# One transfer per tile for the spread C, B, dt and dt*u of a selective scan, with partition = 4 x channel + state

## The chip, the cores and the metric

The kernel runs on one core of one Trainium2 chip. Time is device time in microseconds of one execution, and the median of several executions is compared. The engines of the core are TensorE (PE, matrix products), VectorE (DVE), ScalarE (ACT), GpSimd (POOL), and SyncE (SP), which here only issues DMA transfers. All engines run at the same time, each its own instructions in order, and wait for each other through semaphores. The transfers move data between HBM and SBUF, the on-chip memory of 128 partitions, over 16 DMA engines.

## What is computed

Four layers over x of shape (4, 56, 56, 96). Layers 0 and 1 each contain a selective scan over the 56 x 56 = 3136 positions of an image, in four directions (rows, rows backwards, columns, columns backwards), with 192 channels and 16 states to a channel. Layers 2 and 3 are linear attention and a feed-forward block. The part that matters here is the scan of layer 1 (that of layer 0 differs in constants and in a weight per direction):

```python
x_dbl = jnp.einsum('bkdl,kcd->bkcl', xs, x_proj_w)
dts, Bmat, Cmat = jnp.split(x_dbl, [DTRANK, DTRANK + DSTATE], axis=2)
dts = jnp.einsum('bkrl,kdr->bkdl', dts, dt_w)
...
dt = jax.nn.softplus(dt + dt_bias[None, :, :, None])
dA = jnp.exp(jnp.einsum('bkdl,kdn->lbkdn', dt, A))
dBu = jnp.einsum('bkdl,bknl,bkdl->lbkdn', dt, Bs, u)
...
def step(h, inp):
    dA_l, dBu_l, C_l = inp
    h = dA_l * h + dBu_l
    return (h, jnp.einsum('bkdn,bkn->bkd', h, C_l))
```

For each channel d and state n, h is decayed by exp(dt*A), receives dt*u*B, and is summed over the states with weights C. dt and dt*u depend on the channel and the position only, B and C on the state and the position only.

## The kernel before

The scan works on chunks of 448 positions: 2 layers x 4 images x 4 directions x 7 chunks = 224 chunks. The 192 channels are two halves e of 96 (NE = 2), and a half is three groups g of 32 channels (NG = 3). The 16 states are four quarters q of four states (NQ = 4). A round is one (chunk, e, q), 8 to a chunk and 1792 in all. In a round a tile of 128 partitions holds 32 channels times 4 states, and its three groups g stand beside each other in the free dimension. The partition is 32*s + d for state s (the state is q + 4*s) and channel d.

So dt and dt*u must be copied to four partitions per channel, and B and C to 32 partitions per state. This goes through HBM. `rows` writes the projection, C in rows 0 to 15 and B in rows 16 to 31, into `cf`; `prepare` stores it as `cd` (L547). `park` (L506) stores dt (tile `dtc`) or dt*u (tile `duc`) of a chunk as `dd`, one transfer each. `spread` (L511) fills a tile `dt` or `du` for one e with four transfers of 32 partitions, and `fetch` (L528) fills a tile `cb` with C and B of one q with four more. Each of the four copies C and B of one state to 32 partitions. `cb` has five buffers, `dt` and `du` two each.

A round reads these tiles as follows. ACT makes `da` = exp(dt*A) (L654, three groups, scale by the column `na`). PE spreads B of the quarter into PSUM by a product with the constant `sel` (L597), and DVE multiplies `du` by it for groups 0 and 1 (L695); POOL does group 2 from `cb` (L690). DVE runs the three scans (L702). POOL multiplies by C (`hc`, L744), and PE adds up the four states with the constant `four` (L775). ACT copies the sums to Y (L782) and passes the last column of each scan on (`carry`, L667 and L672).

Beside the scans run lanes of other work (projections, convolutions, layers 2 and 3), one part of a lane at a time in gaps. Their loads (`get` L890, `window` L930) and stores go through SP too. The order on PE, ACT, DVE and POOL is the order of the program text. That of SP's transfers isn't written by hand; the framework's scheduler sets it. SP issues in that order, and a transfer that waits for a semaphore holds all behind it. In `prepare`, o counts rounds before the chunk's first round: `cd` at -9, `dtd` parked at -5, `dud` parked and the first dt spread at -4, the first du at -3, the second du and dt at 0, a fetch at each of -3 to 0.

Of the kernel before, what the change touches and what calls it, by code (L numbers as in the profile page):

```python
# [11 lines left out]
F32 = mybir.dt.float32  # L12
# [4 lines left out]
ALU = mybir.AluOpType  # L17
AX = mybir.AxisListType
# [4 lines left out]
C = 96  # L23
DI = 192
NS = 16
NE = 2
NG = 3
NQ = 4
# [4 lines left out]
CS = 448  # L33
# [48 lines left out]
def _in_blocks(w):  # L82

    u, z = w[..., :DI], w[..., DI:]
    return np.concatenate([u[..., :128], z[..., :128], u[..., 128:], z[..., 128:]], -1)


def lay_out(i):
    i = {k: np.asarray(v) for k, v in i.items()}
    c96, c128, w96, w128, q96, q128 = Cols(C), Cols(128), Cols(C), Cols(128), Cols(C), Cols(128)  # L90
    p0, p1 = "L0_conv_", "L1_conv_"

    for n in ("norm_w", "norm_b", "norm2_w", "norm2_b", "ffn_b2"):
        c96.add("0" + n, i[p0 + n][:, None])
    for n in (
        "dw_b bn1_g bn1_b bn1_m bn1_v pw_b bn2_g bn2_b bn2_m bn2_v ln_g ln_b fus_b fus_ln_g fus_ln_b"
    ).split():
        c96.add("1" + n, i[p1 + n][:, None])
    c96.add("1dw_w", i[p1 + "dw_w"].reshape(C, 9))
    for l in "23":  # L100
        c96.add(l + "bq", i[f"L{l}_attn_bqkv"][:C, None])
        c96.add(l + "bff", i[f"L{l}_attn_bff"][:, None])
        c96.add(l + "b2", i[f"L{l}_ffn_b2"][:, None])
        c128.add(l + "b1", i[f"L{l}_ffn_b1"].reshape(3, 128).T)

    scan = (
        (i[p0 + "ssm_xw"], i[p0 + "ssm_dtw"], i[p0 + "ssm_dtb"], i[p0 + "ssm_Alog"], i[p0 + "ssm_D"]),
        (
            i[p1 + "x_proj_w"],
            i[p1 + "dt_w"],  # L110
            i[p1 + "dt_b"],
            i[p1 + "A_logs"].reshape(4, DI, NS),
            i[p1 + "Ds"].reshape(4, DI),
        ),
    )
    wd = np.zeros((2, 4, 128, WD), np.float32)
    for l, (xw, dw, db, al, dd) in enumerate(scan):
        r = RANK[l]
        for k in range(4):
            t = xw[k].T  # L120
            m = np.zeros((128, NE, 2, 64), np.float32)
            m[:C, :, 0, :32] = np.concatenate([t[:, r + NS :], t[:, r : r + NS]], 1).reshape(NE, C, 32).swapaxes(0, 1)
            m[:C, :, 0, 32 : 32 + r] = t[:, :r].reshape(NE, C, r).swapaxes(0, 1)
            m[:, :, 1, :32] = m[:, :, 1, 32:] = m[:, :, 0, :32]
            wt = np.zeros((128, DI), np.float32)
            wt[32 : 32 + r] = dw[k].T
            bias = np.zeros((128, NE), np.float32)
            bias[:C] = db[k].reshape(NE, C).T
            a = al[k].reshape(NE, NG, 32, 4, NQ).transpose(3, 2, 0, 4, 1).reshape(128, -1)
            wd[l, k] = np.concatenate([m.reshape(128, -1), wt, bias, a], 1)  # L130
        c128.add(f"{l}D", dd.T.reshape(NE, C, 4).swapaxes(0, 1))
    c128.add("0dir", np.broadcast_to(i[p0 + "dir_w"], (128, 4)))
    c128.add("0b1", i[p0 + "ffn_b1"].reshape(3, 128).T)
    for n, v in (
        ("1conv_b", i[p1 + "conv_b"][:, None]),
        ("1conv_w", i[p1 + "conv_w"].reshape(DI, 9)),
        ("1g", i[p1 + "out_norm_g"][:, None]),
        ("1b", i[p1 + "out_norm_b"][:, None]),
    ):
        c128.add(n + "a", v[:128])  # L140
        c128.add(n + "b", v[128:])

    w96.add("0in", _in_blocks(i[p0 + "in_w"].T))
    w96.add("1in", _in_blocks(i[p1 + "in_proj_w"].T))
    w96.add("0w1", i[p0 + "ffn_w1"].T)
    w96.add("1pw", i[p1 + "pw_w"])
    f = i[p1 + "fus_w"].T
    w96.add("1fa", f[:C])
    w96.add("1fb", f[C:])
    w96.add("1out", i[p1 + "out_proj_w"])  # L150
    w = i[p0 + "out_w"].T
    w128.add("0outa", w[:128])
    w128.add("0outb", w[128:])
    w128.add("0w2", i[p0 + "ffn_w2"].T.reshape(3, 128, C).transpose(1, 0, 2))
    for l in "23":
        w96.add(l + "qkv", i[f"L{l}_attn_Wqkv"])
        w96.add(l + "ff", i[f"L{l}_attn_Wff"])
        q96.add(l + "w1", i[f"L{l}_ffn_W1"].T)
        q128.add(l + "w2", i[f"L{l}_ffn_W2"].T.reshape(3, 128, C).transpose(1, 0, 2))
    bqkv = np.stack([i[f"L{l}_attn_bqkv"] for l in "23"])  # L160
    cols = {"c96": c96, "c128": c128, "w96": w96, "w128": w128, "q96": q96, "q128": q128}
    arrays = {"x": np.ascontiguousarray(i["x"]).reshape(NB, L, C), "bqkv": bqkv, "wd": wd}
    arrays.update({k: v.array() for k, v in cols.items()})
    return arrays, {k: v.at for k, v in cols.items()}


class Net:
# [42 lines left out]
    def par(self, group, name):  # L210
        a, n = self.at[group][name]
        return self.tiles[group][:, a : a + n]
# [37 lines left out]
    def setup(self):  # L250
        nc, tc, const = self.nc, self.tc, self.const
        par = self.par
        self.tiles = {}
        for g in ("c96", "c128", "w128"):
            t = const.tile(list(self.aps[g].shape), F32, name=g)
# [8 lines left out]
        make_identity(nc, self.ident)  # L264

        self.four = const.tile([128, 32], F32, name="four")
        nc.vector.tensor_reduce(self.four, self.ident.rearrange("p (s d) -> p d s", s=4), AX.X, ALU.add)
        self.avg96 = const.tile([C, C], F32, name="avg96")
        nc.vector.memset(self.avg96, 1.0 / C)
        self.cen96 = const.tile([C, C], F32, name="cen96")  # L270
# [27 lines left out]
        w = const.tile([128, 4], F32, name="wts")  # L298
        m = const.tile([128, 1], F32, name="wmax")
        d = par("c128", "0dir")  # L300
# [5 lines left out]
        nc.vector.tensor_scalar(w, w, m, None, ALU.mult)  # L306

        self.cscale = const.tile([128, 4], F32, name="cscale")
        nc.vector.memset(self.cscale, 1.0)
        nc.vector.tensor_copy(self.cscale[:NS], w[:NS])  # L310


        self.skip = []
        for l in range(2):
            dv = par("c128", f"{l}D")[:C].rearrange("p (e k) -> p e k", e=NE)
            s = const.tile([C, NE], F32, name=f"dsum{l}")
# [5 lines left out]
            g = const.tile([C, NE, C], F32, name=f"skip{l}")  # L322
# [6 lines left out]
        for n, bias in (("bn1", "1dw_b"), ("bn2", "1pw_b")):  # L329
            s = const.tile([C, 1], F32, name=n + "s")  # L330
            t = const.tile([C, 1], F32, name=n + "t")
# [14 lines left out]
        with tc.tile_pool(name="stage", bufs=1) as st:  # L346

            self.sel = const.tile([128, NQ, 128], BF16, name="sel")
            parts = st.tile([128, 128], F32, name="parts")
            nc.vector.tensor_tensor(parts[:, :32], self.ident[:, 64:96], self.ident[:, 96:], ALU.add)  # L350
            nc.vector.tensor_tensor(parts[:, :32], parts[:, :32], self.ident[:, :32], ALU.add)
            for q in range(NQ):
                nc.vector.tensor_copy(
                    self.sel[:, q].rearrange("p (s d) -> p s d", s=4),
                    parts[:, NS + q : NS + q + 13 : 4].unsqueeze(2).to_broadcast([128, 4, 32]),
                )
            self.some = self.upper(self.tiles["w128"][:, :CS])
            self.minus = const.tile([128, 64], BF16, name="minus")
# [3 lines left out]
            t = st.tile([C, 2, 3, 128], F32, name="q96")  # L362
            nc.scalar.dma_start(t.rearrange("p l m f -> p (l m f)"), self.aps["q96"])
            nc.vector.tensor_copy(self.w1q, t, saturate=False)
            t = st.tile([128, 2, 3, C], F32, name="q128")
            nc.scalar.dma_start(t.rearrange("p l m f -> p (l m f)"), self.aps["q128"])
            nc.vector.tensor_copy(self.w2q, t, saturate=False)
            for n, l in enumerate("23"):
                t = st.tile([128, 3], F8, name="b1s")
                nc.vector.tensor_copy(t, par("c128", l + "b1"), saturate=False)  # L370
                nc.vector.tensor_copy(self.b1q[:, n, :], t)
                t = st.tile([C, 1], F8, name="b2s")
# [4 lines left out]
            t = st.tile(list(self.aps["w96"].shape), F32, name="w96")  # L377
# [15 lines left out]
            for n, l in enumerate("23"):  # L393
                f = st.tile([C, 3 * C], F32, name="qkvf")
                w = par("w96", l + "qkv")
# [9 lines left out]
            t = st.tile([C, C], F32, name="pws")  # L405
# [6 lines left out]
            for n, s in (("a", slice(0, 128)), ("b", slice(128, DI))):  # L412
                rows = s.stop - s.start
                y = self.small("wy" + n, rows, C, (out[:, s], par("w96", "1fb")))
                for l, p in ((self.wyg, "1g"), (self.wyb, "1b")):
                    t = const.tile([rows, C], F32, name="w" + p + n)
# [87 lines left out]
        self.nc.gpsimd.tensor_tensor(in_rows(ch.duc), in_rows(ch.dtc), u[:, :, lo : lo + CS // HS], ALU.mult)  # L504

    def park(self, t):  # L506
        d = self.dram.tile([NE, C, CS], F32, tag="dd", name="dd", bufs=6)
        self.nc.sync.dma_start(d.rearrange("e p t -> p e t"), t)
        return d

    def spread(self, t, d):  # L511

        for s in range(4):
            self.nc.sync.dma_start(t[32 * s : 32 * s + 32], d.rearrange("(g d) t -> d g t", d=32))

    def spread_dt(self, ch, e):
        ch.dt.append(self.sp.tile([128, NG, CS], F32, name="dt"))
# [10 lines left out]
    def fetch(self, ch, q):  # L528

        t = self.sp.tile([128, 2, CS], F32, name="cb", bufs=5)  # L530
        rows = ch.cd.rearrange("(k n) t -> n k t", k=2)
        for s in range(4):
            self.nc.sync.dma_start(t[32 * s : 32 * s + 32], rows[q + 4 * s].partition_broadcast(32))
        ch.cb.append(t)

    def prepare(self, ch, o):
# [835 lines left out]
```

## Time and profile before

| | |
|---|---|
| median of 3 runs | 8356.53 us (8340.41 to 8364.75) |
| profiled execution, its own time | 8364.46 us |
| its span, first to last instruction | 8362.7 us |
| mean granted TensorE clock | 0.898 |
| DMA packets of the SP queue | 942720, 1408.34 MB, 68.2% of 16 engines' span |
| HBM read, written | 1141.42 MB, 268.14 MB |
| SP waiting before L508 for dtc, for duc | 1158.7 us, 1042.4 us |
| SP waiting before L533 for hc (POOL L744) | 383.5 us |

The profile is of one execution. A line of the table of groups gives the source line, the engine, the operation, the tiles written and read, the count, then the busy time in us and the mean duration in ns, then the engine's idle time just before these instructions and what ended most of it. A line of waits names the engine and line that waited, what it waited for, and the total in us, the number of times and the longest. A line of transfers gives the count, the KB of one, and the median of the time from issue to landing.

### The profile page before, as it was taken

The page shows a single profiled execution, that of the slowest core. Times are in us where ns is not written, and L with a number is a line of the kernel's source. Part 1 is how long each engine was busy: PE and PEld are TensorE (multiplying, and loading weights), DVE is VectorE, ACT ScalarE, POOL GpSimd, SP SyncE. Part 2 cuts the span into 40 slices and gives each one's busy share as a digit, 9 for nine tenths or more (in the row PEclk, how much of TensorE's full clock was granted, in tenths as well). Part 3 has the DMA queues.
Part 4 walks back from the last instruction along what each step waited for, and adds up shares of the span by engine and source line. Part 5 has one row for each costly group of instructions (what it writes and reads, how often), then busy time and mean ns, then how long its engine had stood idle before and what let it go on. Part 6 is the DMA issues. An engine that isn't in the chain of part 4 may idle for free. (4 is left out here: it accounts for less than half of the span.)

```text
span 8362.7 us, 119228 instructions
## 1 busy us (share of the span) xinstructions
PE 7469.6 (89%) x33633; PEld 2721.6 (33%) x33633; DVE 7516.6 (90%) x9555; ACT 6109.8 (73%) x12807; POOL 7177.3 (86%) x3991
## 2 busy tenths in 40 slices
PE   7889888898889988898899979988899888998997
PEld 3333233232333223232322323333333333333344
DVE  5999999999998999999998999999999999999921
ACT  5778878776787768786777766777776777767736
POOL 4999989989998999899898998998888888889820
PEclk8899989899999989998898989988899888999986
DMA  5777777678766777677776777676766667666721
GB/s 154 179 188 189 203 179 182 167 175 199 178 174 170 172 188 181 172 177 184 177 175 167 174 185 176 166 170 172 186 166 162 166 173 182 167 160 167 175 57 48
DMA packets 944159, 1417.77 MB, mean 170 GB/s; under 512 B 169410, under 2 KB 936644, under 8 KB 942628
## 3 DMA queue, kind: packets, MB, share of 16 engines
q1 hardware_dynamic: 942720, 1408.34, 68.2%
q8 instruction: 264, 4.33, 0.2%
q14 instruction: 403, 3.30, 0.1%
q10 hardware_dynamic: 772, 1.80, 0.1%
HBM read 1141.42 MB, written 268.14 MB: 169 GB/s over the span
## 5 line engine op out<-in xcount | busy, mean ns | idle before, releaser
L702 DVE TENSOR_TENSOR_SCAN h<-da,h 128x449 f32<-128x449 f32 (+1 forms) x5376 | 5507.1, 1071 | 134.9 <-ACT da L654 79.3
L744 POOL TENSOR_TENSOR hc<-h,cb 128x1344 f32<-128x1344 f32 x1792 | 4884.8, 2726 | 598.8 <-DVE h L702 413.6
L654 ACT ACTIVATE da<-dt,na 128x448 f32<-128x448 f32 x5376 | 3353.1, 632 | 1143.2 <-DVE h L702 1104.4
L695 DVE TENSOR_TENSOR h<-du,b 128x448 f32<-128x448 f32 x3584 | 2019.6, 604 | 182.7 <-PE b L597 112.6
L775 PE MATMUL y<-hc,four 128*32 128x448 f32 x14336 | 1913.0, 609 | 17.8 <-POOL hc L744 17.4
L690 POOL TENSOR_TENSOR h<-du,cb 128x448 f32<-128x448 f32 x1792 | 1754.1, 979 | 141.4 <-DMA cb<-cd 110.1
L762 PE MATMUL y<-w,zeros 128*96 128x448 bf16 x4843 | 1354.0, 397 | 0.0
L597 PE MATMUL b<-cf,sel 128*128 128x448 bf16 x1792 | 680.2, 380 | 631.2 <-DVE h L695 626.6
L762 PEld LDWEIGHTS <-zeros 128*96 128x96 bf16 x4843 | 603.2, 135 | 1111.0 <-issue 965.1
L775 PEld LDWEIGHTS y<-hc,four 128*32 128x32 f32 x14336 | 294.2, 113 | 1182.5 <-issue 660.5
L433 PE MATMUL pp<-U,wd 96*128 96x448 f32 x896 | 664.5, 830 | 12.1 <-DMA U<-u 8.3
L771 PE MATMUL y<-Y,ident 96*96 96x448 f32 x672 | 542.9, 898 | 18.6 <-ACT Y L782 14.3
L919 PE MATMUL ps<-win,dg 64*64 64x220 f32 (+11 forms) x1998 | 547.3, 471 | 0.0
L479 PE MATMUL pp<-cf,wd 12*96 12x448 f32 (+1 forms) x896 | 476.2, 613 | 71.7 <-ACT dtc L489 47.6
L672 ACT COPY carry<-h 128x3 f32<-128x3 f32 x1536 | 301.9, 197 | 282.3 <-DVE h L702 276.2
L504 POOL TENSOR_TENSOR duc<-dtc,U 96x896 f32<-96x896 f32 x224 | 483.1, 2157 | 3.3 <-ACT dtc L491 3.3
L782 ACT COPY Y<-y 96x448 f32<-96x448 f32 x448 | 341.7, 763 | 77.7 <-PE y L775 76.8
L919 PEld LDWEIGHTS ps<-win,dg 64*64 64x64 f32 (+2 forms) x1998 | 239.7, 162 | 321.5 <-issue 289.0
L667 ACT COPY h<-carry 128x3 f32<-128x3 f32 x1536 | 280.2, 182 | 66.3 <-POOL hc L744 63.5
L489 ACT ACTIVATE dtc<-pp,wd 96x448 f32<-96x448 f32 x448 | 281.7, 629 | 31.3 <-PE pp L479 27.4
L597 PEld LDWEIGHTS <-sel 128*128 128x128 bf16 x1792 | 183.8, 103 | 336.1 <-issue 272.7
L827 PEld LDWEIGHTS ps<-avg,w 96*112 96x112 f32 (+2 forms) x1944 | 249.9, 193 | 108.1 <-issue 59.0
(427 smaller groups left out, 5933.9 us busy)
## 6 DMA issues: line engine op xcount, KB each, us to landing
cb<-cd SPq DMA_DIRECT2D x3584, 112.0 KB, 3.9
dt<-dd SPq DMA_DIRECT2D x1792, 168.0 KB, 4.3
du<-dd SPq DMA_DIRECT2D x1792, 168.0 KB, 4.1
dd<-dtc SPq DMA_DIRECT2D x224, 336.0 KB, 3.0
dd<-duc SPq DMA_DIRECT2D x224, 336.0 KB, 3.1
U<-u SPq DMA_DIRECT2D x112, 168.0 KB, 4.7
z<-w SPq DMA_DIRECT2D x56, 224.0 KB, 4.5
u<-w SPq DMA_DIRECT2D x56, 224.0 KB, 3.9
```

The costliest lines, as they stand in the source:

```text
L433: self.nc.tensor.matmul(ch.ps.rearrange("p (a b) -> p a b", b=HS), ch.par.wx[:, e], self.in_order(self.U[e], ch.orient, ch.c * CS, CS), st ...
L504: self.nc.gpsimd.tensor_tensor(in_rows(ch.duc), in_rows(ch.dtc), u[:, :, lo : lo + CS // HS], ALU.mult)
L597: self.nc.tensor.matmul(ps, self.sel[:, q], self.upper(ch.cf), start=True, stop=True)
L654: nc.scalar.activation(da[g][:, INNER], ch.dt[e][:, g], AF.Exp, scale=ch.par.na[:, e, q, g : g + 1])
L690: nc.gpsimd.tensor_tensor(tokens(hs[n])[:, 2], ch.du[e][:, 2], ch.cb[q][:, 1], ALU.mult)
L695: nc.vector.tensor_tensor(tokens(hs[n])[:, g], ch.du[e][:, g], bs[n], ALU.mult)
L702: nc.vector.tensor_tensor_scan(h[:, way], da[g][:, way], h[:, way], 0.0, ALU.mult, ALU.add)
L744: nc.gpsimd.tensor_tensor(hc, tokens(hs[n]), ch.cb[q][:, 0].unsqueeze(1).to_broadcast([128, NG, CS]), ALU.mult,)
L762: self.nc.tensor.matmul(self.y[:C], self.zeros, self.some, start=False, stop=False)
L771: nc.tensor.matmul(o, w, self.in_order(a, ch.orient, ch.c * CS, CS), start=True, stop=False)
L775: nc.tensor.matmul(self.y[32 * n : 32 * n + 32], self.four, hc[:, g], start=n == 3, stop=n == 3 or q == NQ - 1,)
L919: self.nc.tensor.matmul(o[:, a - r0 : e - r0, x0:x1], diag[:, tap], win[:, a + dy - lo : e + dy - lo, x0 + dx : x1 + dx], start=n == 0, st ...
```

## The change

In the tiles of a round the partition becomes 4*d + s. The state of q and s is still q + 4*s. The rows of `cd` are reordered so that those of one q stand together and C and B of one state are neighbours: row 8*q + 2*s is C, row 8*q + 2*s + 1 is B. So the eight rows of one q are one contiguous stretch of HBM, and one transfer repeats it 32 times to fill `cb`. `dd` is stored as [e, channel in group, group, position], so that the three groups of a channel are one contiguous row of 3 x 448 values; one transfer reads each row four times and fills `dt` or `du`. For this, `park` writes with three transfers, one for each group, where it wrote with one. The constants follow the new order: the projection's columns, A, `four`, `sel`, and `cscale`, whose weight must now fall on every second row (only layer 0 uses it, on C).

```diff
-            m[:C, :, 0, :32] = np.concatenate([t[:, r + NS :], t[:, r : r + NS]], 1).reshape(NE, C, 32).swapaxes(0, 1)
+            cb = np.stack([t[:, r + NS :], t[:, r : r + NS]], -1).reshape(NE, C, 4, NQ, 2)
+            m[:C, :, 0, :32] = cb.swapaxes(2, 3).reshape(NE, C, 32).swapaxes(0, 1)
...
-            a = al[k].reshape(NE, NG, 32, 4, NQ).transpose(3, 2, 0, 4, 1).reshape(128, -1)
+            a = al[k].reshape(NE, NG, 32, 4, NQ).transpose(2, 3, 0, 4, 1).reshape(128, -1)
...
-        nc.vector.tensor_reduce(self.four, self.ident.rearrange("p (s d) -> p d s", s=4), AX.X, ALU.add)
+        nc.vector.tensor_reduce(self.four, self.ident.rearrange("p (d s) -> p d s", s=4), AX.X, ALU.add)
...
-        nc.vector.memset(self.cscale, 1.0)
-        nc.vector.tensor_copy(self.cscale[:NS], w[:NS])
+        nc.vector.tensor_reduce(m, self.ident[:, : 2 * NS : 2], AX.X, ALU.add)
+        nc.vector.tensor_scalar(self.cscale, w, m, None, ALU.mult)
+        nc.vector.tensor_scalar(m, m, -1.0, 1.0, ALU.mult, ALU.add)
+        nc.vector.tensor_scalar(self.cscale, self.cscale, m, None, ALU.add)
...
-                    self.sel[:, q].rearrange("p (s d) -> p s d", s=4),
-                    parts[:, NS + q : NS + q + 13 : 4].unsqueeze(2).to_broadcast([128, 4, 32]),
+                    self.sel[:, q].rearrange("p (d s) -> p d s", s=4),
+                    parts[:, 8 * q + 1 : 8 * q + 8 : 2].unsqueeze(1).to_broadcast([128, 32, 4]),
...
     def park(self, t):
-        d = self.dram.tile([NE, C, CS], F32, tag="dd", name="dd", bufs=6)
-        self.nc.sync.dma_start(d.rearrange("e p t -> p e t"), t)
+        d = self.dram.tile([NE, 32, NG, CS], F32, tag="dd", name="dd", bufs=6)
+        for g in range(NG):
+            self.nc.sync.dma_start(d[:, :, g].rearrange("e d t -> d e t"), t[32 * g : 32 * g + 32])
         return d
 
     def spread(self, t, d):
 
-        for s in range(4):
-            self.nc.sync.dma_start(t[32 * s : 32 * s + 32], d.rearrange("(g d) t -> d g t", d=32))
+        rows = d.rearrange("d g t -> d (g t)").unsqueeze(1).to_broadcast([32, 4, NG * CS])
+        self.nc.sync.dma_start(t.rearrange("p g t -> p (g t)"), rows)
...
         t = self.sp.tile([128, 2, CS], F32, name="cb", bufs=5)
-        rows = ch.cd.rearrange("(k n) t -> n k t", k=2)
-        for s in range(4):
-            self.nc.sync.dma_start(t[32 * s : 32 * s + 32], rows[q + 4 * s].partition_broadcast(32))
+        rows = ch.cd[8 * q : 8 * q + 8].rearrange("(s k) t -> s (k t)", k=2)
+        self.nc.sync.dma_start(
+            t.rearrange("p k t -> p (k t)"), rows.unsqueeze(0).to_broadcast([32, 4, 2 * CS])
+        )
         ch.cb.append(t)
```

## The prediction

> **What bounds the kernel now.** I read the page from the top: busy shares first, then the groups of part 5, the DMA issues of part 6, and after that the waits and the SP queue's timeline at the worst wait. The first two parts name the engine that sets the pace.
>
> ```profile
> PE 7469.6 (89%) x33633; PEld 2721.6 (33%) x33633; DVE 7516.6 (90%) x9555; ACT 6109.8 (73%) x12807; POOL 7177.3 (86%) x3991
> ...
> L702 DVE TENSOR_TENSOR_SCAN h<-da,h 128x449 f32<-128x449 f32 (+1 forms) x5376 | 5507.1, 1071 | 134.9 <-ACT da L654 79.3
> L744 POOL TENSOR_TENSOR hc<-h,cb 128x1344 f32<-128x1344 f32 x1792 | 4884.8, 2726 | 598.8 <-DVE h L702 413.6
> ...
> L695 DVE TENSOR_TENSOR h<-du,b 128x448 f32<-128x448 f32 x3584 | 2019.6, 604 | 182.7 <-PE b L597 112.6
> ...
> L690 POOL TENSOR_TENSOR h<-du,cb 128x448 f32<-128x448 f32 x1792 | 1754.1, 979 | 141.4 <-DMA cb<-cd 110.1
> ...
> cb<-cd SPq DMA_DIRECT2D x3584, 112.0 KB, 3.9
> dt<-dd SPq DMA_DIRECT2D x1792, 168.0 KB, 4.3
> du<-dd SPq DMA_DIRECT2D x1792, 168.0 KB, 4.1
> dd<-dtc SPq DMA_DIRECT2D x224, 336.0 KB, 3.0
> ```
>
> The scan stage has 1792 rounds. A round without a wait runs 4.0 us on DVE (two products of 0.6 us and three scans of 1.07 us, their ends overlapping), so 1792 x 4.0 = 7170 us of the 8363 us are DVE work of the scan alone. The view by windows says how much of the stage is idle:
>
> ```profile
> 200.00:2000.00 1800.00, 1595.13 (x7163) 546.43 (x7155) 1725.83 (x2153) 1393.93 (x2828) 1668.01 (x925) 0.90 0.74 183
> 2000.00:4000.00 2000.00, 1770.90 (x7919) 596.62 (x7911) 1898.22 (x2367) 1498.12 (x3006) 1837.18 (x1014) 0.91 0.73 180
> 4000.00:6000.00 2000.00, 1804.57 (x8171) 639.40 (x8172) 1881.74 (x2377) 1472.29 (x3121) 1802.62 (x999) 0.90 0.71 174
> 6000.00:7900.00 1900.00, 1761.08 (x8063) 653.65 (x8061) 1770.01 (x2262) 1374.75 (x3063) 1672.89 (x925) 0.91 0.69 169
> ```
>
> The columns are length, then busy time of PE, PE's weight loads, DVE, ACT and POOL, the clock, the DMA share and GB/s. DVE's busy time sums to 7275.8 of 7700 us, so DVE idles 424 us there. No change to transfers can win more than that, and only the part of it that ends on a transfer. The view of waits shows that part:
>
> ```profile
> DVE h L695 <- PE b L597: 112.6, 143, 4.6
> POOL h L690 <- DMA cb<-cd: 110.1, 28, 18.6
> ...
> DVE h L702 <- ACT da L654: 79.3, 165, 2.1
> ...
> DVE h L702 <- POOL h L690: 53.2, 26, 10.1
> ...
> DVE h L695 <- DMA du<-dd: 34.4, 9, 15.6
> ```
>
> DVE waits for du itself 34.4 us (15.6 of it once, at the first round), and 53.2 us for POOL's third product, which in its long cases had waited for cb. Three of those cases (10.1, 10.1 and 9.6 us, each followed by 2.0 us) come to 36 us; others at L702 are 1 us waits behind L1016 and L1017 on POOL. So transfers own some 70 us, at most 88 us, of DVE's idle time.
>
> Why are they late? One of the three cases, on SP and on POOL:
>
> ```profile
> 3532.66 0.47 SPq L930 DMA_DIRECT2D win<-m  x1
> 3533.23 1.95 SPq L514 DMA_DIRECT2D dt<-dd  x4
> 3535.27 1.78 SPq L533 DMA_DIRECT2D cb<-cd  x4
> ...
> 3540.63 0.98 POOL L690 TENSOR_TENSOR h<-du,cb 128x448 f32<-128x448 f32 x1 [13.25 <-DMA cb<-cd]
> ```
>
> SP issued nothing from 3517.4 to 3532.7: the window load of L930 at its head waited for a buffer. Only then came dt and cb, eight issues. POOL had been idle since 3527.4: 5.3 us before SP was free and 7.9 us after it, of which eight issues of 0.43 us are 3.4. The larger part is the queue's order and the landing, the smaller the number of issues.
>
> [...] of the packets of 1792 bytes a third take 70 to 75 ns, and from 200 to 7900 us the median is 113 ns and the 90th percentile 149[...]. [...] the scan takes 1054 to 1096 ns in every stage. So fewer bytes in flight buy nothing on DVE or POOL.
>
> **The change part by part.**
>
> *Issues.* Fetch: 3584 become 896. Spreads of dt and du: 2 x 1792 become 2 x 448. Park: 2 x 224 become 2 x 672. SP's 9000 transfers become 9000 - 2688 - 2688 + 896 = 4520. At the median of 0.43 us each (L533 and L514 by line), SP has 1.9 ms less to issue. That is not time on the path: SP also sits waiting for dtc and duc (1158.7 and 1042.4 us before L508). It counts only where a queue has built up.
>
> *Landing of a tile.* Now: the first to the last issue of the four is 1.29 to 1.6 us at the median for all but the first cb (which SP splits around a park), plus 3.9 to 4.3 us, so 5.2 to 5.9 us. After: packets of 3584 and 5376 bytes, eight on each engine. At the rate of the fast 1792-byte packet (74 ns) to that of the slow (149 ns), cb takes 8 x 148 to 298 ns = 1.2 to 2.4 us, dt and du 1.8 to 3.6 us. In today's 3.9 and 4.2 us are 4 and 6 packets of 114 ns, 0.46 and 0.68 us, so 3.45 to 3.5 us remain, part of it queueing behind other transfers. Together cb 4.65 to 5.85 us, dt and du 5.3 to 7.1 us: between 0.6 us earlier and 1.6 us later than now. I take no difference for cb and 0.5 us later for dt and du[...].
>
> *What slack hides that.* For each of the 224 chunks I set the last issue of a tile plus 4.2 us against the start of its first reader. Median slack is 4.5 us for the first cb, 4.6 for the second, 5.4, then 2.1 for the fourth; 6.6 for the first du, 11.4 for the second, over 7 for dt. So half a microsecond either way is hidden: summing what falls short, tiles that land 1 us later cost 20 us in all, 2 us 61, 3 us 142.
>
> *Backlogs.* Here issues count. At the first round DVE starts at 111.8 us after a run of 12 issues for du, dt and cb; three in their place save about 5 us. At 1683 us DVE waits 6.5 us for du, of which one quarter had been issued before the block and three after it; whole, it goes before: 4 us, as cb is next late. The three 12 us cases each keep the blocked window but have 6 issues fewer before the late cb, 6 x 0.43 = 2.6 us, 8 us in all. Near 1070, 2058, 3022 and 4000 us ten loads of the next lane and twelve spreads fill the queue; DVE waits there 1 to 2 us three times in a row, and L1016 on POOL waits for w; I take 3 us each, 12 us. The waits of 2.7 us near 1992 and 4926 us and small ones: 6 us. Sum 5 + 4 + 8 + 12 + 6 = 35 us. Bounds: 15 us if the lane's cases are POOL's own work, 80 us if SP's order also changes so that dt and cb pass the window load.
>
> *Park.* Two more issues before the last lands, 2 x 0.45 = 0.9 us later, and the spread behind it waits for three transfers. Queued behind on SP: dt, du and cb. The three spreads that follow now take 12 x 0.45 us and then 3, so this is covered; uncovered it is below the 20 us named above.
>
> *Semaphores.* Readers wait for one transfer where they waited for four: L690 has 2808 separate semaphore instructions on POOL, L695 1650 on DVE. They run while the engine is still busy: in the stage DVE's idle stretches under 100 ns sum to 2.5 us, POOL's to 2.4. Nothing gained.
>
> *Constants.* The new cscale is four small DVE operations in place of two in the set-up, under 1 us; `four` and `sel` keep shapes and counts, so L775 (609 ns) and L597 (380 ns) stay. Per-partition `na` and `cf` keep their form.
>
> Sum: the profiled execution has 8364.5 us (span 8362.7), so it becomes 8329; the median of the runs is 8 us below that execution, so 8321.
>
> **The rivals.**
> *Hidden anyway.* The long waits are order, not number; SP is idle half the time, and the median tile has 2 to 6 us of slack. Then only start and stray cases remain, 0 to 20 us: 8345. Against it speak the crowded stretches.
> *Slower: one transfer lands later than four.* Place: the fourth cb tile, slack 2.1 us. If [...]each tile waits for its slowest engine behind another 672 KB transfer, tiles land 2 us or more later: +61 us, at 3 us +142. It decides from about 2 us, where the loss of 61 us exceeds the 35 us won by 25 us. At 3 us, less the 35 won: 8357 + 107 = 8464. Against it: the range above ends at 1.6 us.
> *Not 16 engines.* [...]the 1.03 GB of the spreads and fetches (3584 x 112 KB + 3584 x 168 KB) through 4 engines at 24 GB/s (1792 bytes in 74 ns) would take 10.6 ms, beyond the whole span. [...]
>
> **How the numbers follow.** 0.3% is 25 us, about what a measurement of this kernel can tell. The 35 us case where it shows (25 to 80 us won, 8276 to 8331): 0.48. Hidden: 0.29. Slower: 0.21, and 0.02 for few engines. The predicted time is 8321. The likeliest case's own range, by its bounds of 15 and 80 us, is 8276 to 8341. The whole range goes to 8262, as all of DVE's waits for transfers (88 us) and a little of POOL's could go, and to 8420, which leaves out about half of the slower case.
>
> **What would show it.** SP transfers near 4520; cb, dt and du at 448 and 672 KB, landing in 4 to 6.5 us; the DMA share down from 68% to 45 to 60%; DVE's wait for du near 15 us and POOL's for cb near 60; durations unchanged. The window load still heads SP's queue in the three long cases. I am wrong if waits for cb spread over many chunks, if landings pass 7 us, or if DVE's idle time moves without transfers.

## The result and the profile after

The changed kernel takes 8281.9 us at the median (8280.05 to 8300.63, 4 runs) against 8360.64 us for the kernel before (4 runs): ratio 0.9918, 95% interval 0.9898 to 0.9938, so 0.82% faster (the quotient of the two medians, 0.9906, lies in the interval). The forecast was 8321 us, faster by 0.42%, with a range of 8262 to 8420. The profiled execution has 8300.6 us with a span of 8298.9 us, 63.8 us shorter than that of the kernel before.

The page of the changed kernel, its busy shares, its costliest groups and its transfers (the lines of the source have moved down by three to five: L695 is now the third product on POOL, L700 the products on DVE, L707 the scan, L749 the product with C):

```profile
PE 7409.9 (89%) x33633; PEld 2704.3 (33%) x33633; DVE 7512.5 (91%) x9557; ACT 6105.7 (74%) x12807; POOL 7176.7 (86%) x3991
...
q1 hardware_dynamic: 526976, 1408.05, 52.6%
...
L707 DVE TENSOR_TENSOR_SCAN h<-da,h 128x449 f32<-128x449 f32 (+1 forms) x5376 | 5501.9, 1070 | 93.5 <-ACT da L659 78.0
L749 POOL TENSOR_TENSOR hc<-h,cb 128x1344 f32<-128x1344 f32 x1792 | 4885.3, 2726 | 637.1 <-DVE h L707 502.8
...
L695 POOL TENSOR_TENSOR h<-du,cb 128x448 f32<-128x448 f32 x1792 | 1754.9, 979 | 44.8 <-DMA du<-dd 19.9
...
cb<-cd SPq DMA_DIRECT2D x896, 448.0 KB, 4.3
dt<-dd SPq DMA_DIRECT2D x448, 672.0 KB, 5.0
du<-dd SPq DMA_DIRECT2D x448, 672.0 KB, 5.6
dd<-dtc SPq DMA_DIRECT2D x672, 112.0 KB, 2.0
```

DVE and POOL work no less: DVE's busy time is 7512.5 us where it was 7516.6, POOL's 7176.7 where it was 7177.3, and a scan still takes 1.07 us. What changed is what stands after the last bar of a line, the idle time. That of L695 on POOL fell from 141.4 to 44.8 us. The same bytes keep the DMA engines busy for 52.6% of the span, not 68.2%.

PE's recorded busy time did fall, by 59.7 us, and this hints at a rival: the granted clock. It was 0.907 in the profiled execution where it was 0.898 before. In the four runs of the changed kernel it was 0.905 to 0.909, in the runs of the kernel before that stand beside the experiments below 0.896 to 0.904, and among those the quickest had one of the highest clocks (8319.91 us at 0.904) and the slowest one of the lowest (8376.52 us at 0.897). In the profiled pair the clock explains little, as DVE waits for PE's spread of B as long as before (112.6 us):

```profile
DVE h L700 <- PE b L602: 111.5, 135, 5.4
```

How much of the difference of the medians goes with the clock, and whether the clock is its cause or follows from it, stays open. No run held the clock fixed.

The waits of DVE in the changed kernel (engine and line, what it waited for, total, times, longest):

```profile
DVE h L700 <- DMA du<-dd: 22.0, 5, 17.9
...
DVE h L707 <- POOL h L695: 13.0, 15, 2.4
```

These answer to 34.4 and 53.2 us before. POOL itself waited 110.1 us for cb; now that line reads

```profile
POOL h L695 <- DMA cb<-cd: 0.3, 1, 0.3
```

and the wait at its first round, 19.9 us, is put down to du. In the stage from 200 to 7900 us (third of the busy times)

```profile
200.00:7900.00 7700.00, 6926.64 (x31603) 2441.48 (x31600) 7338.21 (x9241) 5784.09 (x12130) 7042.09 (x3895) 0.92 0.55 178
```

DVE's busy time is 7338.2 us of 7700 where it was 7275.8, so its idle time fell by 62.4 us, from 424.2 to 361.8. That is nearly the whole difference of the spans. Attributing each idle stretch of DVE in this stage to its releaser, du's own share falls from 18.8 to 4.1 us and that of POOL's third product from 53.7 to 13.4 us: 55 of the 62 us.

The three places where POOL had waited 13 us for cb behind a blocked window load are gone. SP at the second of them, in the changed kernel:

```profile
3505.28 0.51 SPq L518 DMA_DIRECT2D du<-dd  x1
3505.89 0.55 SPq L518 DMA_DIRECT2D dt<-dd  x1
3507.60 4.14 SPq L536 DMA_DIRECT2D cb<-cd  x2
3518.94 1.27 SPq L512 DMA_DIRECT2D dd<-dtc  x3
3525.58 0.30 SPq L512 DMA_DIRECT2D dd<-duc  x1
3525.98 0.49 SPq L935 DMA_DIRECT2D win<-m  x1
```

The second du, the second dt and the fetches of cb are issued first; the window load comes 18 us after the fetches begin, between the parts of a park. Before, the same load stood between du and dt and held dt and cb for 15 us. The change touches no window load. The scheduler that sets SP's order placed it elsewhere once the other transfers had changed.

So there are two candidates that the result alone doesn't tell apart: the order of SP's queue, which the change altered by accident, and the transfers themselves, fewer, larger, and over all 128 partitions.

### The profile page after: what moved, and what is told of

Its sections match the earlier page's. It is cut to its first block, busy times and chain, and to the rows that moved or that the text cites. A ratio compares the mean times of both kernels' runs of the same rounds, so it can differ in the third digit from the quotient of the medians.

```text
span 8298.9 us, 112395 instructions
## 1 busy us (share of the span) xinstructions
PE 7409.9 (89%) x33633; PEld 2704.3 (33%) x33633; DVE 7512.5 (91%) x9557; ACT 6105.7 (74%) x12807; POOL 7176.7 (86%) x3991
## 3 DMA queue, kind: packets, MB, share of 16 engines
q1 hardware_dynamic: 526976, 1408.05, 52.6%
## 5 line engine op out<-in xcount | busy, mean ns | idle before, releaser
L707 DVE TENSOR_TENSOR_SCAN h<-da,h 128x449 f32<-128x449 f32 (+1 forms) x5376 | 5501.9, 1070 | 93.5 <-ACT da L659 78.0
L749 POOL TENSOR_TENSOR hc<-h,cb 128x1344 f32<-128x1344 f32 x1792 | 4885.3, 2726 | 637.1 <-DVE h L707 502.8
L700 DVE TENSOR_TENSOR h<-du,b 128x448 f32<-128x448 f32 x3584 | 2017.1, 603 | 162.8 <-PE b L602 111.5
L780 PE MATMUL y<-hc,four 128*32 128x448 f32 x14336 | 1889.5, 602 | 19.0 <-POOL hc L749 18.5
L695 POOL TENSOR_TENSOR h<-du,cb 128x448 f32<-128x448 f32 x1792 | 1754.9, 979 | 44.8 <-DMA du<-dd 19.9
L767 PE MATMUL y<-w,zeros 128*96 128x448 bf16 x4843 | 1335.3, 393 | 0.0
L602 PE MATMUL b<-cf,sel 128*128 128x448 bf16 x1792 | 674.7, 377 | 632.2 <-DVE h L700 626.1
L780 PEld LDWEIGHTS y<-hc,four 128*32 128x32 f32 x14336 | 293.9, 112 | 1172.2 <-issue 676.7
L602 PEld LDWEIGHTS <-sel 128*128 128x128 bf16 x1792 | 183.3, 102 | 331.5 <-issue 267.6
```

Of the source, the lines that this page charges most:

```text
L602: self.nc.tensor.matmul(ps, self.sel[:, q], self.upper(ch.cf), start=True, stop=True)
L695: nc.gpsimd.tensor_tensor(tokens(hs[n])[:, 2], ch.du[e][:, 2], ch.cb[q][:, 1], ALU.mult)
L700: nc.vector.tensor_tensor(tokens(hs[n])[:, g], ch.du[e][:, g], bs[n], ALU.mult)
L707: nc.vector.tensor_tensor_scan(h[:, way], da[g][:, way], h[:, way], 0.0, ALU.mult, ALU.add)
L749: nc.gpsimd.tensor_tensor(hc, tokens(hs[n]), ch.cb[q][:, 0].unsqueeze(1).to_broadcast([128, NG, CS]), ALU.mult,)
L767: self.nc.tensor.matmul(self.y[:C], self.zeros, self.some, start=False, stop=False)
```

## The experiments

Every ratio is to the kernel before, with its 95% interval.

### Four issues for a tile again, but over 128 partitions

```diff
-        self.nc.sync.dma_start(t.rearrange("p g t -> p (g t)"), rows)
+        w = t.rearrange("p g t -> p (g t)")
+        for j in range(0, NG * CS, 336):
+            self.nc.sync.dma_start(w[:, j : j + 336], rows[:, :, j : j + 336])
```

`fetch` is cut in the same way into four times 224 columns.

> The changed kernel, but each tile of cb, dt and du is filled by four transfers again, each over all 128 partitions and a quarter of the columns (896 or 1344 bytes a row). SP issues 9896 transfers, more than before the change. If the gain came from the number of issues in SP's queue, it is lost: 8330 to 8370 us, and POOL waits for cb 60 us or more again. If it came from filling all 128 partitions at once ([...]shorter landing), it stays: 8275 to 8305 us.

Measured: 1.0013 (0.9998 to 1.0027). The whole win is lost, as the first of the two guesses had it. Its transfers and the waits at the third product:

```profile
cb<-cd SPq DMA_DIRECT2D x3584, 112.0 KB, 2.6
dt<-dd SPq DMA_DIRECT2D x1792, 168.0 KB, 2.8
du<-dd SPq DMA_DIRECT2D x1792, 168.0 KB, 2.9
```

```profile
POOL h L697 <- DMA cb<-cd: 88.0, 34, 19.9
```

```profile
DVE h L709 <- POOL h L697: 64.2, 55, 2.9
```

A transfer lands in 2.6 us where the kernel before needed 3.9, of as many bytes, and still POOL waits for cb and DVE for POOL. So a quicker single transfer doesn't hold the win when SP issues 9896 of them. DVE's wait also has another form: 55 short ones, none above 2.9 us, so the three long blocks are absent here too. This points to backlog in the queue. But number and price of the issues rose together: one of these takes SP 0.60 us at the median, where one of the kernel before took 0.43. The run doesn't separate the two.

### SP in the order of the program text, before and after

```diff
-    with tc.manual_schedule(engines={E.PE, E.Activation, E.DVE, E.Pool}):
+    with tc.manual_schedule(engines={E.PE, E.Activation, E.DVE, E.Pool, E.SP}):
```

The kernel before with this edit:

> The kernel before, with SP's transfers too in the order of the program text instead of the scheduler's. If the gain is that blocked window loads no longer stand ahead of dt and cb, text order alone gives most of it with the same 9000 transfers: 8290 to 8325 us and no wait of 10 us for cb. If it is the number of issues or the landing time, nothing comes of it: 8345 to 8375 us.

The changed kernel with it:

> The changed kernel, with SP in the order of the program text. If order is all, this equals e2 within 15 us. If the number of issues also counts at equal order, it stands 20 us or more below e2: 8265 to 8295 us.

Measured: 1.0039 (1.0017 to 1.0060) for the kernel before, 0.9989 (0.9980 to 0.9999) for the changed one. The guesses about text order missed: it helps neither kernel, and the kernel before is slower than either guess. Of the pair, the changed kernel is the faster by 43 us at the medians, in the direction of the second guess, but far from its 8265 to 8295 us. The traces in text order say why. First the changed kernel, on SP and then on DVE:

```profile
3502.43 19.36 SPq L935 DMA_DIRECT2D win<-m  x2
3521.89 0.55 SPq L518 DMA_DIRECT2D du<-dd  x1
3522.53 0.55 SPq L518 DMA_DIRECT2D dt<-dd  x1
3523.14 0.59 SPq L536 DMA_DIRECT2D cb<-cd  x1
```

```profile
3532.41 1.09 DVE L707 TENSOR_TENSOR_SCAN h<-da,h 128x449 f32<-128x449 f32 x1 [12.00 <-POOL h L695]
```

Then the kernel before, at the same place:

```profile
3532.38 17.54 SPq L930 DMA_DIRECT2D win<-m  x2
3550.03 1.94 SPq L514 DMA_DIRECT2D du<-dd  x4
```

```profile
3561.71 1.09 DVE L702 TENSOR_TENSOR_SCAN h<-da,h 128x449 f32<-128x449 f32 x1 [12.64 <-POOL h L690]
```

In text order the window load stands ahead of du, dt and cb in both kernels, and with one issue a tile the block costs nearly as much as with four: 12.0 us against 12.6 here, and 11.2 to 12.0 against 12.6 to 13.3 over the three places of this kind. So few issues don't cure a blocked head. At this common order the change still wins 0.5% (0.9989 to 1.0039).

### A fourth window buffer, so that nothing blocks

```diff
-NWIN = 3
+NWIN = 4
```

The kernel before with it:

> The kernel before with a fourth buffer for the window tile (NWIN 4), so that L930 need not wait for a buffer; SP still issues 9000 transfers in the scheduler's order. If the three waits of 12 us for cb behind a blocked window load were a main part of what the change won, they vanish and the time falls by 30 to 45 us, to 8305 to 8325 us at a before of 8350. If the number of issues is all, the time stays within 15 us of before.

The changed kernel with it:

> The changed kernel with the same fourth window buffer. If the change had already removed these waits by another way, nothing is left to win: within 10 us of the changed kernel, ratio to before 0.990 to 0.993. If blocked window loads still cost something, a further 15 to 40 us.

Measured: 0.9957 (0.9941 to 0.9972) and 0.9919 (0.9892 to 0.9946). The kernel before wins 0.43% from a buffer alone, some half of what the change won, and in the range expected. In its trace:

```profile
DVE h L702 <- POOL h L690: 18.4, 21, 2.4
DVE h L695 <- DMA du<-dd: 31.9, 9, 15.6
```

```profile
POOL h L690 <- DMA cb<-cd: 54.4, 20, 19.0
```

DVE's wait for POOL's third product falls from 53.2 to 18.4 us; that is 35 of the 38 us by which the median fell. POOL's wait for cb is halved from 110.1 us (19.0 of what is left is at the first round), and DVE's for du hardly changes in total. The changed kernel gains nothing further that shows, as had been guessed: its order had removed these blocks. What remains between the two, 0.9919 to 0.9957, is 0.4%, some 32 us. It may belong to the transfers, but the two still differ in SP's order.

### Text order and the fourth buffer together

Both edits above at once, on the changed kernel and on the kernel before:

> The changed kernel, SP in text order, with a fourth window buffer. If the blocked window loads are why text order loses the win (e3), it comes back: ratio to before 0.990 to 0.994. If text order costs by parks or other stores at the queue's head, it stays at 0.997 to 1.000.

> The kernel before, SP in text order, with a fourth window buffer. The blocked loads are gone for both sides, so e9 minus e8 is what fewer and larger transfers are worth at one order of SP: 20 to 45 us, ratio 0.995 to 0.999. If they are worth nothing without the blocks, e9 equals e8.

Measured: 0.9925 (0.9903 to 0.9947) and 0.9967 (0.9957 to 0.9977). Both are as expected. With the buffer, text order is as good as the scheduler's for the changed kernel within the intervals, so the blocked load was what was wrong with it. The two ratios differ by 0.42%, 35 us, at one order of SP and without blocks (the medians by 42). This repeats the 0.4% of the pair before it. POOL's waits for cb differ, here first for the kernel before and then for the changed one:

```profile
POOL h L690 <- DMA cb<-cd: 79.6, 35, 24.9
```

```profile
POOL h L695 <- DMA cb<-cd: 29.1, 3, 23.5
```

Apart from the first round (24.9 and 23.5 us) that is 54.7 us in 34 waits against 5.6 us in two. But little of this reaches DVE, which sets the pace. Its own waits, in the same order:

```profile
DVE h L695 <- DMA du<-dd: 40.9, 9, 20.9
DVE h L702 <- POOL h L690: 15.7, 18, 2.4
```

```profile
DVE h L700 <- DMA du<-dd: 25.7, 6, 20.3
DVE h L707 <- POOL h L695: 11.4, 13, 2.4
```

For POOL's third product DVE waits only 4.3 us less. For du, apart from the first round, it waits 5.4 us instead of 20.0. So some 19 of the 35 us are seen to end on du or on POOL; where the rest lies isn't shown. The granted clock differs here as well (0.902 and 0.906 on average over the runs).

### Which tile's issues count

The cut into four columns of the first experiment, in `fetch` alone and in `spread` alone:

> The changed kernel with only the fetch of cb in four transfers (quarters of the columns, all 128 partitions), 7208 transfers. By the queue theory cb is the tile with least slack, so this loses most of the win: ratio 0.995 to 1.001. By a theory that the large dt and du spreads matter, little is lost: 0.991 to 0.994.

> The changed kernel with only the spreads of dt and du in four transfers (quarters of the columns), cb in one, 7208 transfers as well. By the queue theory these stand ahead of cb in SP's queue but cb is one issue: about half of the win stays, ratio 0.993 to 0.997. By a theory of total issues, the same as e6.

Measured: 0.9947 (0.9926 to 0.9967) and 0.9935 (0.9916 to 0.9953). Both have 7208 transfers. The first falls between its two guesses, the second into its own. Both ratios lie above the changed kernel's 0.9918, but the intervals overlap its interval and each other: that each alone costs some of the win, or the fetch more than the spread, isn't shown. Together they cost all of it (1.0013).

### Two transfers: halves of the partitions or halves of the columns

Halves of the partitions (`fetch` likewise, with its 16 copies for each half):

```diff
-        self.nc.sync.dma_start(t.rearrange("p g t -> p (g t)"), rows)
+        w = t.rearrange("p g t -> p (g t)")
+        for j in range(2):
+            self.nc.sync.dma_start(w[64 * j : 64 * j + 64], rows[16 * j : 16 * j + 16])
```

> The changed kernel with each tile in two transfers of 64 partitions, packets as large as in the changed kernel, 6312 transfers on SP. By the queue theory a small loss against the changed kernel, 5 to 20 us: 0.993 to 0.996. [...]

Halves of the columns are the first experiment's edit with 672 and 448 columns:

> The changed kernel with each tile in two transfers over all 128 partitions and half of the columns, 6312 transfers as in e10. By the queue theory the same time as e10 within 10 us: 0.993 to 0.996. [...]

Measured: 0.9995 (0.9981 to 1.0008) for partitions, 0.9930 (0.9908 to 0.9952) for columns. The same 6312 issues and the same bytes give all of the loss in one case and next to none in the other; the guess of 0.993 to 0.996, which goes by the number of issues, holds for the columns and not for the partitions. Their transfers, partitions first:

```profile
q1 hardware_dynamic: 555648, 1408.17, 66.8%
```

```profile
cb<-cd SPq DMA_DIRECT2D x1792, 224.0 KB, 6.5
dt<-dd SPq DMA_DIRECT2D x896, 336.0 KB, 5.5
```

and columns:

```profile
q1 hardware_dynamic: 785024, 1408.17, 54.0%
```

```profile
cb<-cd SPq DMA_DIRECT2D x1792, 224.0 KB, 4.0
dt<-dd SPq DMA_DIRECT2D x896, 336.0 KB, 4.5
```

A half tile of cb over 64 partitions lands 2.5 us later than a half of its columns, one of dt 1.0 us later, and the DMA engines are busy nearly as long as before the change (66.8% of the span, 68.2% before). By the packet records, a packet of 5376 bytes has a median of 206 ns in the changed kernel and 355 ns here, one of 3584 bytes 140 and 232 ns. Why packets take longer into 64 partitions isn't shown. But the time of this run has a second cause: the scheduler placed a window load between the two fetches of one cb tile, and waits behind it are back, though of 6 us where the kernel before had 10. First DVE's waits, then SP:

```profile
DVE h L709 <- POOL h L697: 38.1, 24, 6.1
```

```profile
3522.41 0.52 SPq L540 DMA_DIRECT2D cb<-cd  x1
3536.20 0.48 SPq L937 DMA_DIRECT2D win<-m  x1
3536.74 0.59 SPq L540 DMA_DIRECT2D cb<-cd  x1
```

So the halves of 64 partitions were run once more without blocks, in text order and with the fourth buffer:

> The two transfers of 64 partitions of e10, with SP in text order and four window buffers, so at the order of e8 (0.9925) and e9 (0.9967) and without blocked window loads. If [...]the landing time are what separates e8 from e9, this stands at e9: 0.995 to 0.998. If the number of issues separates them (4520, here 6312, 9000), it stands near e8, 0.992 to 0.9945, and what e10 lost was the order that the scheduler gave it.

Measured: 0.9950 (0.9934 to 0.9967), between the changed kernel (0.9925) and the kernel before (0.9967) at this order, and its interval overlaps both. Its waits are close to those of the kernel before:

```profile
POOL h L697 <- DMA cb<-cd: 74.3, 22, 24.8
DVE h L702 <- DMA du<-dd: 43.3, 10, 20.6
```

POOL waits 74.3 us for cb (79.6 before, 29.1 changed), and DVE 22.7 us for du apart from the first round (20.0 before, 5.4 changed). The halves of the columns, with as many issues, leave POOL at its third product only the wait at the first round:

```profile
POOL h L697 <- DMA cb<-cd: 19.2, 1, 19.2
```

So the waits come back with the transfers of 64 partitions and not with the number of issues, as far as runs at two different orders of SP can tell. Late landing fits this for cb (6.5 us at the median against 4.0) but not plainly for du, whose transfers land in 5.5 us here and in the changed kernel at this order. How the 35 us divide between landing and issues isn't settled: four issues over all partitions lost as well.

No version was faster than the changed kernel beyond its interval.

## Why the prediction was right, and where its sum was off

The direction and the range held, and so did the bound: DVE's waits for transfers own 70 to 88 us, and in the stage 55 us of them are gone. The route held only in part. Some 36 of the 55 us fell at the three places where the window load no longer blocks SP's queue, and the prediction had named as a sign that it still would. POOL's wait for cb, forecast near 60 us, is 0.3 us (with 19.9 at the first round now put down to du); DVE's for du, forecast near 15, is 22.0. So about half of the gain, which was twice the forecast, comes from an order of the queue that nobody chose, and that is luck. The forecast of 35 us is close to what the change is worth with no blocks and at one order of SP, 35 us; by the traces only some 19 of these are waits of the forecast kind.

- *Issues and durations.* SP issues 4520 transfers, as worked out. L780 and L602 keep their durations within 2% (602 ns after 609, 377 after 380), the constants (four operations for `cscale`, 0.73 us in all) and the semaphores cost nothing that shows.
- *Landing.* Forecast: cb 4.65 to 5.85 us, dt and du 5.3 to 7.1; measured 4.3, 5.0 and 5.6, so cb and dt land sooner than the whole range. My estimate had allowed 74 to 149 ns for 1792 bytes; the median packets are 140 ns for 3584 bytes and 206 for 5376, a little below the fast end of the allowance (two and three times 74). Eight packets on each engine was my estimate, an even split of 128 over 16 engines; the split itself isn't shown. Where the 128 packets of a tile stand apart from those of other tiles of its size, they take 1.97 us from first to last at the median for cb (forecast 1.2 to 2.4) and 2.7 for dt and du (forecast 1.8 to 3.6), with some 12 under way at once on average. The DMA share is 52.6%, inside 45 to 60%.
- *The three 12 us cases.* This is the term that was mis-sized: "each keep the blocked window but have 6 issues fewer before the late cb", 8 us in all. In fact the block itself went, as SP's order changed, and 36 us were won. The prediction had this only as its outer bound of 80 us. The runs in text order show what its assumption would have been worth: with the block kept in both kernels, the three cases cost DVE 44.6 us before and 40.4 after (each with the 2.0 us that follow it), so 4 of the 8 us would have come.
- *The start.* Forecast 5 us won; DVE's first round begins at 115.4 us where it began at 111.8, so 3.6 us were lost. The park of du in three parts was issued between stores and loads of the start, the last part at 106.04 us, and du only at 109.43; before, the whole park was out at 90.19 and du began at 105.13. The prediction called the park covered; here it was not.
- *Backlogs.* Near 1683 us the wait for du of 6.5 us is gone (4 forecast), but not because the tile goes out whole before the block: the window load is no longer there, and the fourth buffer removes this wait too with the transfers as before. The waits for du near 1085 and 1992 us are gone; new are one of 1.2 us for POOL at 1663 us and one of 1.5 us for du at 3909. Of the 55 us in the stage, 19 lie outside the three cases, where the sum had 4 + 12 + 6 = 22. By the pairs without blocks, backlog and landing together are worth 32 to 35 us. This term was about right in size.
- *Rivals.* "Hidden anyway" is excluded by the interval. "One transfer lands later than four" is refuted by the landing times above. The slack of the fourth cb tile (last issue plus 4.2 us, set against the start of POOL's third product) has a median of 7.8 us, where the trace before gives 3.2 in this way and the prediction had read 2.1. "Not 16 engines" would have taken 10.6 ms by the prediction's estimate (four engines, 1792 bytes in 74 ns), longer than the whole span.

## What to carry to other kernels

A transfer queue is an engine with an order: look for the transfer that waits at its head, and who stands behind it. Here a window load at the head held dt and cb for 15 us in the kernel before, and one more buffer for a tile that the change never touched was worth half of what the whole new layout won. When a change alters the number of transfers under a scheduler, compare both traces for moved transfers before the gain is put down to the transfers, and repeat the comparison at one fixed order. Look also at the granted clock of both sides.

A layout in which a tile's source is contiguous for each partition lets one transfer fill all partitions. Here a cb tile then lands 4.3 us after its one issue, where the last of four issues came 1.3 to 1.6 us after the first and landed 3.9 us later. Four transfers of 128 partitions lost the win, two of 64 lost it in part or whole, and two of 128 kept most of it (0.9930).

## What was not expected of the hardware

An issue to SP isn't one price: the transfers of dt, du and cb over 128 partitions take 0.51 to 0.53 us of SP at the median, those over 32 partitions took 0.43, and the quarters of the columns over 128 partitions 0.60. Other transfers land later beside the large ones: the stores of z (224 KB) in 6.2 us where they needed 4.5, those of u in 5.8 instead of 3.9, though the DMA engines are less busy. With the same bytes in quarters of the columns the stores of z land in 2.7 us, in halves in 5.5. None of these stores was waited for on DVE in the changed kernel.
